# A sigmoid recurrence in chunks of two lengths, with its additions on VectorE and a last attention tile in two unequal parts

## The chip, the cores and the metric

The kernel runs on one core of a Trainium2 chip. The metric is the device time of one execution in microseconds (us), taken as the median of several runs. Engines are named as the profile names them: PE (TensorE), DVE (VectorE), ACT (ScalarE), POOL (GpSimd) and SP (SyncE, which here only issues transfers).

## What is computed

The input is a tensor of 4 batches, 128 channels and 64 x 64 = 4096 positions, all in float32. Layer 0 is a group norm and a full attention over the positions. Layer 1 treats the positions as tokens: a layer norm and a causal attention, then a layer norm and a recurrent block. Each adds its result to its input. The part that the change is about is the end:

```python
x = x + attn0(group_norm(x))                 # 4096 x 4096 scores for each batch
t = tokens(x)                                # (4, 4096, 128)
t = t + causal_attn(layer_norm(t))
Wx = layer_norm(t) @ W.T                     # normalised over all 4 x 4096 tokens
Wx = (Wx - mean) * rsqrt(var + 1e-5) * gamma + beta
def step(yt, wx_t):                          # over the 4096 tokens, y0 = 0
    yt = sigmoid(wx_t + yt @ V.T)
    return yt, yt
t = t + ys
```

## The kernel before

**Attention.** The batches are worked through one after the other, and each batch in its two layers. A layer is cut into 8 tiles of 512 queries. A tile is made of units: a unit takes 256 keys (two blocks of 128), computes their scores on PE (`ps`, L888 in layer 1), the exponentials on ACT (`s`, L901), a running sum of them on DVE (`total`, L929) and their product with the values on PE (`av`, L932). The product of a unit follows the score of the next one in PE's order. Work that belongs to other tiles is put between units by hand: `finish` divides by the sum, projects (`po`) and adds the input; `ffn` then normalises the tokens (`pt_f`, `rstd_f`), multiplies by the recurrent block's weight (`pw_f`, `w_f`), and ACT writes the product into `WX` (L752). Each of these is a generator that does one piece between two units; where it yields, the next unit comes first. In causal tiles POOL sets the upper triangle of the diagonal blocks to zero (L904).

In the last layer of the last batch the order of the tiles is 0, 1, 2, 4, 5, 6, 7, 3, and tile 3 is done in two halves of 256 queries (`LAST = 3`). When all is done, the statistics over all tokens are put together (`fmv`, L981), and from them a `gain` and a `bias`.

**Recurrence.** The 4096 steps are cut into chunks of `CHUNK = 32`, which run side by side: 128 chunks of each batch are the columns of one matmul. The start of a chunk isn't known, so each first runs the last `WARM = 12` steps of the chunk before it from a value of 0.5 into `first`; at the end `ok` compares the value so reached with the one that the neighbour computed, and only where they differ by more than 2e-6 a second, general kernel runs. A chain makes 12 + 32 = 44 steps. There are two chains, of two batches each, so a step of a chain has 256 columns: a matmul with `FV` (L1020) adds to PSUM, where DVE has written `gain * Wx` ahead of it (`seed`, L1010, four steps at once into one of two buffers of the chain), and a sigmoid on ACT (L1021) writes the result into `first` or over `WX`.

`residual` (L1025) adds `WX` to the kept input of the recurrent block (`Y` for batches 0 to 2, `X` for batch 3). The tokens of a chunk lie 32 elements apart there. POOL does it for batches 0 and 1 and most of batch 2 while the steps run; DVE does the last 8 steps of batch 2 and all of batch 3 after them. Then 8 stores of 1 MB go out, half on SP's queue and half on ACT's.

Of the kernel before, what the change touches and what calls it, by code (L numbers as in the profile page):

```python
# [463 lines left out]
CHUNK = 32  # L464
# [5 lines left out]
BL = 4  # L470
LAST = 3
# [3 lines left out]
def fast_kernel(  # L475
# [14 lines left out]
    NP = N // (2 * P)  # L490
    NC = N // CHUNK
    G = 4
    assert C == P and 2 * CQ == P and N % QT == 0 and NC == P
# [60 lines left out]

    WXp = [wxpool.tile([P, 2, CHUNK, NC], F32, name=f"WX{g}") for g in range(B // 2)]
    WX = [WXp[b // 2][:, b % 2] for b in range(B)]
# [6 lines left out]
    with ExitStack() as actx:  # L563
# [172 lines left out]
        def ffn(b, c, off, w):  # L736
            name = f"f_{b}_{c}_{off}"
            cols = ds(c * QT + off, w)
            src = X2[b][:, cols]
            if b < len(kept):  # L740
                nc.sync.dma_start(out=kept[b][:, cols], in_=src)
            yield
            _, _, rstd = deviations(src, 1e-5, name)
            yield
            rb = spread(rstd, name)
            pw = misc(f"pw_{name}")[:, :w]
            nc.tensor.matmul(pw, lhsT=FWc, rhs=src, start=True, stop=True)  # L747
            if off == 0:
                wt[b, c] = tmp.tile([P, QT], F32, tag="w", name=f"w_{name}")
            part = wt[b, c][:, ds(off, w)]  # L750
            nc.vector.tensor_tensor(part, pw, rb, ALU.mult)  # L751
            nc.scalar.copy(  # L752
                WX[b][:, :, ds((c * QT + off) // CHUNK, w // CHUNK)].rearrange("p l s -> p s l"),
                part.rearrange("p (s l) -> p s l", l=CHUNK),
            )
            if off + w == QT:
                nc.vector.bn_stats(stats_f[:, b * NQ + c, :], wt.pop((b, c)))
            yield

        def finish(b, layer, c, off, w, av, total):  # L760
# [24 lines left out]
            yield  # L785
            yield
# [12 lines left out]
        units, following = [], {}  # L799
        for b in range(B):  # L800
            for layer in range(2):
                order = list(range(NQ))
                if (b, layer) == (B - 1, 1):
                    order.append(order.pop(LAST))
                following.update({(b, layer, c): d for c, d in zip(order, order[1:])})
                for c in order:
                    halves = [(0, QT // 2), (QT // 2, QT // 2)] if (b, layer, c) == (B - 1, 1, order[-1]) else [(0, QT)]
                    for off, w in halves:
                        n = (c * QT + off + w) // (2 * P) if layer else NP
                        units += [(b, layer, c, off, w, u, n) for u in range(n)]  # L810
# [22 lines left out]
        def begin_tile(b, layer, c):  # L833

            if layer == 0:
                if c == 0 and b:
                    for k in range(NQ):
                        whole(("k0", b, k))
                    put(("q0", b, 0), query0(b, 0))
                if c == 1 and b == 0:  # L840
                    put(("m1",), merge1())
                if c == 3 and 0 < b < B - 1:
                    for k in range(NQ):
                        whole(("f", b - 1, k, 0))
                    load_x(b + 1)
                if c == (5 if b else 2) and b + 1 < B:
                    put(("gn", b + 1), gn_stats(b + 1))
                if c == NQ - 1:
                    put(("q1", b, 0), after(b, 0))
                whole(("q0", b, c))  # L850
                if c + 1 < NQ:
                    put(("q0", b, c + 1), query0(b, c + 1))
            else:
                if c == 0 and b + 1 < B:
                    whole(("gn", b + 1))
                    for k in range(NQ):
                        put(("k0", b + 1, k), keys0(b + 1, k))
                whole(("q1", b, c))
                if (b, 1, c) in following:
                    d = following[b, 1, c]  # L860
                    todo.insert(0, ("q1", b, d))
                    made["q1", b, d] = after(b, d)
# [9 lines left out]
        def score(i):  # L872
# [11 lines left out]
            first = [max(j0 + h, 0) * P if layer else 0 for h in range(2)]  # L884
            for h in range(2):
# [12 lines left out]
            for h in range(2 if layer else 0):  # L898
# [3 lines left out]
                if j0 >= 0:  # L902
# [7 lines left out]
        def product(i):  # L910
# [7 lines left out]
            both = first[0] == first[1]  # L918
            if u == 0:
                if not both:  # L920
                    nc.vector.memset(total[:, 1, : first[1]], 0.0)
                for h in (slice(0, 2),) if both else range(2):
                    f = 0 if both else first[h]
                    nc.vector.tensor_copy(total[:, h, f:w], s[:, h, f:w])
            else:
                for h in (slice(0, 2),) if both else range(2):
                    f = 0 if both else first[h]
                    t = total[:, h, f:w]
                    nc.vector.tensor_tensor(t, t, s[:, h, f:w], ALU.add)  # L929
            V = V1[b] if layer else V0[b]  # L930
            for h in range(2):
                nc.tensor.matmul(  # L932
                    av[:, first[h] : w], lhsT=V[:, 2 * u + h, :], rhs=s[:, h, first[h] : w],
                    start=u == 0 and h == 0, stop=u == n - 1 and h == 1,
# [6 lines left out]
            if u == n - 1:  # L941
# [28 lines left out]
    with ExitStack() as fctx:  # L970
# [20 lines left out]
        nil = small.tile([P, QT], F32R, name="nil")  # L991
        nc.vector.memset(nil.bitcast(F32), 0.0)
        first = [small.tile([P, 2, NC], F32, name=f"first{g}") for g in range(B // 2)]
        for g in range(B // 2):
            nc.vector.memset(first[g], 0.5)
        steps = list(range(CHUNK - WARM, CHUNK)) + list(range(CHUNK))
        nk = len(steps) // BL
        where = {}

        def seed(g, k):  # L1000
            ps = where[g, k] = ps_y.tile([P, BL, 2, NC], F32, tag=f"y{g}", name=f"py{g}_{k}")
            if k < 2:
                for j in range(0, BL, 2):
                    nc.tensor.matmul(
                        ps[:, j : j + 2].rearrange("p j h s -> p (j h s)"), lhsT=nil[:, :P], rhs=nil,
                        start=True, stop=True,
                    )
            j0, lo = steps[k * BL], int(k * BL < WARM)
            for js in [slice(j, j + 1) for j in range(BL)] if k == 0 else [slice(0, BL)]:
                nc.vector.tensor_scalar(  # L1010
                    ps[:, js, :, lo:].rearrange("p j h s -> p h j s"),
                    WXp[g][:, :, j0 + js.start : j0 + js.stop, : NC - lo], gain, None, ALU.mult,
                )

        def advance(g, k, j):
            n, lo = k * BL + j, int(k * BL < WARM)
            dst = first[g][:, :, 1:] if lo else WXp[g][:, :, steps[n], :]
            y = dst if lo else first[g] if n == WARM else WXp[g][:, :, steps[n] - 1, :]
            ps = where[g, k][:, j, :, lo:]
            nc.tensor.matmul(ps, lhsT=FV, rhs=y, start=False, stop=True, skip_group_check=True)  # L1020
            nc.scalar.activation(dst, ps, AF.Sigmoid, bias=bias)  # L1021

        def residual(eng, b, ls, cols=slice(0, NC)):
            xj = X[b].rearrange("p (s l) -> p l s", l=CHUNK)[:, ls, cols]
            eng.tensor_tensor(xj, xj, WX[b][:, ls, cols], ALU.add)  # L1025

        for k in range(2):
            for g in range(B // 2):
                seed(g, k)
        for k in range(nk):  # L1030
            for j in range(BL):
                for g in range(B // 2):
                    advance(g, k, j)
            if k == WARM // BL - 1:
                for g in range(B // 2):
                    nc.vector.memset(first[g][:, :, 0:1], 0.0)
            for g in range(B // 2 if k + 2 < nk else 0):
                seed(g, k + 2)
            if k * BL >= WARM:
                ls = slice(steps[k * BL], steps[k * BL] + BL)  # L1040
                for b in range(3 if k < nk - 2 else 2):
                    residual(nc.gpsimd, b, ls)
        residual(nc.vector, 2, slice(CHUNK - 2 * BL, CHUNK))
        for h in range(2):
            residual(nc.vector, 3, slice(0, CHUNK), ts(h, NC // 2))
        for b in range(B):
            for h in range(2):
                cols = ts(h, N // 2)
                (nc.scalar if h else nc.sync).dma_start(out=out[b, :, cols], in_=X[b][:, cols])
# [4 lines left out]
        ok = small.tile([P, B, NC], F32, name="ok")  # L1054
        nc.vector.memset(ok, 0.0)
        for b in range(B):
            nc.vector.tensor_tensor(
                ok[:, b, 1:], first[b // 2][:, b % 2, 1:], WX[b][:, CHUNK - 1, : NC - 1], ALU.subtract
            )
# [3 lines left out]
        nc.vector.tensor_reduce(good[:, 0:1], ok.rearrange("p b s -> p (b s)"), AX.X, ALU.min)  # L1063
# [3 lines left out]
        pf = ps_y.tile([P, BL, 2, NC], F32, tag="y0", name="pflag")[:, 0, 0, :]  # L1067
# [52 lines left out]
```

## Time and profile before

| | |
|---|---|
| median of 3 runs | 2593.09 us (2592.93 to 2595.2) |
| profiled execution | 2594.39 us, of which the span is 2592.4 us |
| last product of attention | 2489.0 us |
| gain ready | 2505.5 us |
| first step of the recurrence | 2508.57 us |
| last sigmoid | 2565.1 us |
| last addition of `residual` | 2578.0 us |
| additions on POOL | 22 of 128x512, 1599 ns each |
| additions on DVE | 1 of 128x1024, 2 of 128x2048 |

Places in time are microseconds from the start of the span of the profiled execution. A duration is that of one instruction by the profiler; "x8" means eight of them. Two records make one float32 matmul. In the timeline the last column in brackets is the engine's idle time ahead of the instruction and what ended it.

### The profile page before, as it was taken

Reading aid. Unit: us, or ns where it says so; the run is one execution under the profiler, and the core shown is the slowest. Engines: PE = TensorE matmul, PEld = TensorE weight load, DVE = VectorE, ACT = ScalarE, POOL = GpSimd, SP = SyncE. Lnnn points to the kernel's source line nnn. Section 1 sums busy time; section 2 is a strip of 40 time slices with the busy share of each in tenths; the row PEclk is TensorE's granted clock in tenths of the full one; section 3 lists DMA queues with packets and bytes.
Section 4 is the critical chain, followed back from the end, with each engine's and each line's share of the span. In section 5 each row is a group of like instructions: output and inputs, shape, how many; then the busy total and the mean of one; then the engine's idle time right before and its main releaser. Section 6 shows DMA issues by size and latency. Waiting matters only on the chain.

```text
span 2592.4 us, 21739 instructions
## 1 busy us (share of the span) xinstructions
PE 2519.8 (97%) x7372; PEld 1345.1 (52%) x7372; DVE 1760.3 (68%) x3513; ACT 1139.7 (44%) x1386; POOL 219.7 (8%) x297
## 2 busy tenths in 40 slices
PE   7999999999999999999999999999999999999975
PEld 4555554444555555444555555444455555544552
DVE  7776667567867667666876666765786766776564
ACT  4444444444444444444444444444444444344444
POOL 2010001101000100010100010110100000000005
PEclk9999999999999999999999999999999999999988
DMA  2000000000100000000100000000010000000013
GB/s 72 1 0 1 0 1 13 9 4 4 37 0 1 0 1 5 13 5 8 37 0 1 1 0 1 13 9 5 5 37 0 1 1 1 0 1 1 0 65 131
DMA packets 11943, 31.28 MB, mean 12 GB/s; under 512 B 2096, under 2 KB 2864, under 8 KB 10032
## 3 DMA queue, kind: packets, MB, share of 16 engines
q1 hardware_dynamic: 8928, 24.12, 2.6%
q10 hardware_dynamic: 2896, 5.71, 0.6%
q8 instruction: 59, 0.97, 0.2%
q14 instruction: 60, 0.49, 0.1%
HBM read 15.14 MB, written 14.68 MB: 12 GB/s over the span
## 4 chain that ended last, share of the span: by engine, by line
PE 89%; DVE 6%; issue 2%; ACT 1%; POOL 1%; DMA 0%; SPq 0%; POOLq 0%; ACTq 0%; DVEq 0%
PE av L932 48%; PE ps L895 17%; PE ps L888 17%; PE po L788 2%; DVE total L929 1%; PE py L1020 1%; PE pq L730 1%; PE pk L649 1%; POOL rstd_f L561 1%; PE pw_f L747 1%; ACT WX L1021 1%; PE pt L688 1%; DVE lst_f L692 0%; PE pt L665 0%; DVE w_f L751 0%
## 5 line engine op out<-in xcount | busy, mean ns | idle before, releaser
L929 DVE TENSOR_TENSOR total<-total,s 128x1024 f32<-128x1024 f32 (+4 forms) x802 | 881.6, 1103 | 553.4 <-ACT s L897 308.9
L932 PE MATMUL av<-s,WX 128*128 128x512 f32 x2048 | 964.4, 593 | 3.4 <-ACT s L897 3.4
L897 ACT ACTIVATE s<-ps,shift 128x1024 f32<-128x1024 f32 x512 | 569.2, 1114 | 772.9 <-PE ps L895 749.0
L895 PE MATMUL ps<-q,K 128*128 128x512 f32 x2048 | 759.7, 493 | 2.1 <-DVE K L660 1.5
L901 ACT ACTIVATE s<-ps,zero,R 128x512 f32<-128x512 f32 (+1 forms) x590 | 399.9, 729 | 458.9 <-PE ps L888 458.3
L932 PEld LDWEIGHTS av<-s,WX 128*128 128x128 f32 x2048 | 382.2, 189 | 312.0 <-issue 270.0
L895 PEld LDWEIGHTS ps<-q,K 128*128 128x128 f32 x2048 | 386.7, 189 | 291.0 <-issue 236.3
L932 PE MATMUL av<-s,V 128*128 128x512 f32 (+3 forms) x1180 | 504.7, 549 | 0.6 <-ACT s L901 0.6
L888 PE MATMUL ps<-q,X 128*128 128x512 f32 (+3 forms) x1180 | 501.9, 548 | 0.0
L888 PEld LDWEIGHTS ps<-q,X 128*128 128x128 f32 x1180 | 222.6, 190 | 239.7 <-issue 228.2
L932 PEld LDWEIGHTS av<-s,V 128*128 128x128 f32 x1180 | 218.8, 191 | 226.1 <-issue 201.6
L561 POOL TENSOR_TENSOR rstd<-rstd,mhalf 128x4 f32<-128x4 f32 x32 | 32.7, 1022 | 1015.5 <-DVE rstd L560 1015.5
L904 POOL TENSOR_SCALAR_AFFINE_SELECT s<-s 128x128 f32<-128x128 f32 x128 | 46.5, 367 | 523.0 <-ACT s L901 522.4
L646 POOL TENSOR_SCALAR X<-X,B0v 128x512 f32<-128x512 f32 x32 | 59.6, 1865 | 243.8 <-DVE xg L644 238.1
L794 DVE SCALAR_TENSOR_TENSOR X<-po,X 128x512 f32<-128x512 f32 (+1 forms) x65 | 44.1, 678 | 51.3 <-PE po L788 50.9
L752 ACT COPY WX<-w_f 128x512 f32<-128x512 f32 (+1 forms) x33 | 35.3, 1069 | 93.1 <-DVE w_f L751 93.1
L561 POOL TENSOR_TENSOR rstd_f<-rstd_f,mhalf 128x4 f32<-128x4 f32 (+1 forms) x33 | 36.1, 1094 | 398.6 <-DVE rstd_f L560 398.6
L721 DVE TENSOR_SCALAR V<-pt,lmv,rstd 128x128 f32<-128x128 f32 x128 | 43.7, 404 | 35.8 <-POOL rstd L561 35.8
L788 PE MATMUL po<-o,W1v 128*128 128x512 f32 (+1 forms) x66 | 34.4, 604 | 16.1 <-DVE o L782 16.1
L679 DVE TENSOR_TENSOR q<-QR,qh 64x512 fp32r<-64x512 f32 x64 | 43.9, 685 | 6.3 <-PE ps L895 5.7
L765 DVE TENSOR_TENSOR t<-total 128x512 f32<-128x512 f32 (+1 forms) x65 | 44.5, 684 | 4.5 <-PE pfw L605 2.5
L782 DVE SCALAR_TENSOR_TENSOR o<-rb,av 128x512 f32<-128x512 f32 (+1 forms) x65 | 43.9, 675 | 4.4 <-DVE rb L780 0.5
(124 smaller groups left out, 1312.5 us busy)
## 6 DMA issues: line engine op xcount, KB each, us to landing
X<-in_x SPq DMA_DIRECT2D x28, 256.0 KB, 5.5
kept<-X SPq DMA_DIRECT2D x24, 256.0 KB, 2.0
Y<-kept SPq DMA_DIRECT2D x6, 1024.0 KB, 7.6
out<-Y SPq DMA_DIRECT2D x3, 1024.0 KB, 9.7
out<-Y ACTq DMA_DIRECT2D x3, 1024.0 KB, 10.2
X<-in_x ACTq DMA_DIRECT2D x4, 256.0 KB, 5.6
out<-X SPq DMA_DIRECT2D x1, 1024.0 KB, 16.1
out<-X ACTq DMA_DIRECT2D x1, 1024.0 KB, 12.6
```

Of the source, the lines that this page charges most:

```text
L561: nc.gpsimd.tensor_tensor(dst, dst, mhalf[:, :n], ALU.pow)
L646: nc.gpsimd.tensor_scalar(xt, xt, B0v, None, ALU.add)
L765: nc.vector.tensor_tensor(t, total[:, 0, :w], total[:, 1, :w], ALU.add)
L788: nc.tensor.matmul(po, lhsT=W1v if layer else W0v, rhs=o, start=True, stop=True)
L794: nc.vector.scalar_tensor_tensor(dst, po, 1.0 / GUARD, xt, ALU.mult, ALU.add)
L888: nc.tensor.matmul(ps[:, h, first[h] : w], lhsT=lhsT, rhs=q[:, off + first[h] : off + w], start=True, stop=True,)
L895: nc.tensor.matmul(ps[:, h, :], lhsT=lhsT, rhs=q[:, k, :], start=k == 0, stop=k == 1)
L897: nc.scalar.activation(s, ps, AF.Exp, bias=shift)
L901: nc.scalar.activation(part, ps[:, h, first[h] : w], AF.Exp, scale=scale, bias=zero)
L904: nc.gpsimd.affine_select(out=edge, in_=edge, pattern=[[1, P]], base=0, channel_multiplier=-1, compare_op=ALU.is_ge, fill=0.0,)
L929: nc.vector.tensor_tensor(t, t, s[:, h, f:w], ALU.add)
L932: nc.tensor.matmul(av[:, first[h] : w], lhsT=V[:, 2 * u + h, :], rhs=s[:, h, first[h] : w], start=u == 0 and h == 0, stop=u == n - 1 and h ...
```

## The change

- Batches 0 and 1 are now cut into chunks of 16 steps, batches 2 and 3 still into chunks of 32. There are three chains: batch 0 alone (256 chunks, 12 + 16 = 28 steps), batch 1 alone (the same), and batches 2 and 3 together (2 x 128 chunks, 44 steps). After the 28th step the two batches of the third chain make their steps separately, with 128 columns each.
- `seed` writes two steps at once for the first two chains and four for the third; the first one isn't cut into single steps any more.
- All additions of `residual` are on DVE: four steps of batches 0 and 1 after each fourth step, eight steps of batches 2 and 3 at a time later, and the last eight in two pieces of four.
- The stores of batches 0 and 1 are issued on SP as soon as their additions are done; those of batches 2 and 3 at the end, half on SP and half on ACT.
- The tiles of the last layer run in their natural order, and the last one (tile 7) is split into 384 and 128 queries. A part can have an odd number of key blocks, so its last unit may have one block. For a part narrower than 512 `finish` yields five times ahead of `po` instead of twice.
- `nil` (zeros, which open the PSUM banks) is made once at the start with 128 columns and read four times over; the memsets of `first` and `ok` move from DVE to POOL.

```diff
-CHUNK = 32
+CHUNK = (16, 16, 32, 32)
-BL = 4
-LAST = 3
+LAST = 384
...
-            yield
-            yield
+            for _ in range(2 if w == QT else 5):
+                yield
             po = misc(f"po_{name}")[:, :w]
...
-                order = list(range(NQ))
-                if (b, layer) == (B - 1, 1):
-                    order.append(order.pop(LAST))
...
+                for c in range(NQ):
+                    parts = [(0, LAST), (LAST, QT - LAST)] if (b, layer, c) == (B - 1, 1, NQ - 1) else [(0, QT)]
+                    for off, w in parts:
+                        n = (c * QT + off + w) // P if layer else NB
+                        units += [(b, layer, c, off, w, u, n) for u in range((n + 1) // 2)]
...
+        chains = (((0,), 2), ((1,), 2), ((2, 3), 4))
...
+            nc.vector.tensor_scalar(
+                ps[:, :, :, lo:].rearrange("p j h s -> p h j s"), src[:, :, j0 : j0 + bl, : NC[b] - lo],
+                gain, None, ALU.mult,
+            )
...
+            parts = [slice(h, h + 1) for h in range(2)] if n >= len(steps[0]) else [slice(0, len(bs))]
+            for hs in parts:
...
+                nc.tensor.matmul(ps, lhsT=FV, rhs=y, start=False, stop=True, skip_group_check=True)
+                nc.scalar.activation(dst, ps, AF.Sigmoid, bias=bias)
+
+        def residual(b, l, n):
+            xj = X[b].rearrange("p (s l) -> p l s", l=CHUNK[b])[:, l : l + n, :]
+            nc.vector.tensor_tensor(xj, xj, WX[b][:, l : l + n, :], ALU.add)
+
+        def store(b, h):
+            (nc.scalar if h and b > 1 else nc.sync).dma_start(out=out[b, :, ts(h, N // 2)], in_=X[b][:, ts(h, N // 2)])
...
-            for g in range(B // 2 if k + 2 < nk else 0):
-                seed(g, k + 2)
-            if k * BL >= WARM:
-                ls = slice(steps[k * BL], steps[k * BL] + BL)
-                for b in range(3 if k < nk - 2 else 2):
-                    residual(nc.gpsimd, b, ls)
-        residual(nc.vector, 2, slice(CHUNK - 2 * BL, CHUNK))
-        for h in range(2):
-            residual(nc.vector, 3, slice(0, CHUNK), ts(h, NC // 2))
...
+        late = [(b, l) for l in range(0, CHUNK[2] - 8, 8) for b in (2, 3)]
+        for n in range(len(steps[2])):
+            for g in range(3):
+                advance(g, n)
...
+            for g, (_, bl) in enumerate(chains):
+                if (n + 1) % bl == 0:
+                    seed(g, (n + 1) // bl + 1)
+            if WARM < n < last and (n + 1) % 4 == 0:
+                for b in range(2):
+                    residual(b, n - WARM - 3, 4)
+                if n == last - 1:
+                    for b in range(2):
+                        for h in range(2):
+                            store(b, h)
+            elif n >= last and late and WARM + late[0][1] + 8 <= n:
+                residual(*late.pop(0), 8)
+        for b, l in late:
+            residual(b, l, 8)
+        for l in (CHUNK[2] - 8, CHUNK[2] - 4):
+            for b in (2, 3):
+                residual(b, l, 4)
+        for b in (2, 3):
+            for h in range(2):
+                store(b, h)
```

## The prediction

> **What bounds the kernel now.** I read the page first, then a table of busy time by stage, then the chain of waits and the timeline of the last 110 us.
>
> ```profile
> PE 2519.8 (97%) x7372; PEld 1345.1 (52%) x7372; DVE 1760.3 (68%) x3513; ACT 1139.7 (44%) x1386; POOL 219.7 (8%) x297
> ```
>
> TensorE (PE) is busy 97% of the span, in attention, which the change leaves alone up to the last tile. What it touches lies in the stages after 2460 us (columns: stage, length, busy time of PE, weight loads, DVE, ACT, POOL, clock, DMA share, GB/s):
>
> ```profile
> 2460.00:2489.00 29.00, 26.42 (x118) 21.93 (x116) 19.96 (x62) 14.86 (x28) 2.68 (x6) 0.94 0.00 1
> 2489.00:2508.50 19.50, 6.52 (x15) 3.81 (x14) 14.84 (x59) 1.55 (x4) 1.96 (x3) 0.65 0.54 215
> 2508.50:2565.10 56.60, 52.73 (x176) 27.13 (x176) 25.06 (x23) 41.13 (x87) 31.07 (x20) 0.97 0.00 0
> 2565.10:2578.00 12.90, 0.26 (x2) 0.00 (x0) 12.88 (x6) 0.47 (x1) 3.23 (x2) 0.61 0.81 335
> 2578.00:2588.00 10.00, 0.59 (x2) 0.50 (x2) 2.62 (x8) 0.00 (x0) 0.00 (x0) 0.50 0.99 406
> ```
>
> The stages are: end of attention; its epilogue on DVE; 44 steps of the recurrence; what is left of the additions on DVE (12.88 of 12.90 us busy); the rest of the stores, with DMA full. The end follows at 2592.4. In the chain of waits a step looks like this:
>
> ```profile
> 2526.76 0.71 PE py L1020 x2
> 2527.47 0.02 issue
> 2527.49 0.48 ACT WX L1021
> 2527.98 0.04 issue
> 2528.02 0.71 PE py L1020 x2
> ```
>
> One step costs 1.26 us, a matmul and a sigmoid in turn; two chains alternate in it, so ACT is used 2 x 0.475 = 0.95 us of 1.26. 44 x 1.26 = 55.4. Last the timeline behind the steps:
>
> ```profile
> 2565.12 1.85 DVE L1057 TENSOR_TENSOR ok<-first,WX 128x127 f32<-128x127 f32 x2 [7.64 <-ACT WX L1021]
> 2565.17 3.23 POOL L1025 TENSOR_TENSOR Y<-Y,WX 128x512 f32<-128x512 f32 x2 [1.93 <-ACT WX L1021]
> 2566.86 3.81 SPq L1049 DMA_DIRECT2D out<-Y  x3
> ...
> 2566.89 3.41 DVE L1025 TENSOR_TENSOR Y<-Y,WX 128x1024 f32<-128x1024 f32 x1
> 2570.13 7.85 DVE L1025 TENSOR_TENSOR X<-X,WX 128x2048 f32<-128x2048 f32 x2
> ```
>
> Two additions of 2048 elements took 7.85 us, **1.9 ns an element**; the one of 1024, counted from 2568.4 when POOL's ended, took 1.7 to 1.9. This price decides the case.
>
> **What the Trainium skill says.** "SBUF — State Buffer", Who interferes with whom: a DVE instruction with two SBUF inputs and a POOL one that reads SBUF shut each other out. The trace agrees: the two small `ok` subtractions took 1.85 us beside POOL's addition, and two later ones 0.50. So additions moved from POOL must be paid on DVE, but nothing blocks them there. The same page, The DMA port swizzle, says that SBUF lines have 16 bytes and each access to a new line costs extra; both strides of the additions (64 and 128 bytes) then cost alike. The trace agrees on 64 bytes for a read, without DMA beside it:
>
> ```profile
> L775 DVE TENSOR_REDUCE z<-side 32x16 f32<-32x64 f32 x63 | 15.1, 239 | 1.4
> L775 DVE TENSOR_REDUCE z<-side 32x8 f32<-32x32 f32 x2 | 0.3, 172 | 0.0
> ```
>
> (239 - 172) / 32 = 2.1 ns an element, where the contiguous reduction of L769 pays (673 - 402) / 256 = 1.06. "TensorE: Matmul & The Clock Gate", LDWEIGHTS: a load of 128 columns takes 128 / 1.2 = 107 ns; its records here last 190 ns but may overlap, since four 128-wide transposes came in 0.44 us. Same page, What's actually happening: after some 3.4 us idle PE runs at half clock. The clock of 0.65 in the epilogue agrees.
>
> **The change part by part.** Times are against the span of the profiled run.
>
> 1. *Last tile in 384 and 128.* PE's columns stay the same: a unit (two 128-row blocks, scores and products) takes 3.44 us at 512 columns, 1.72 at 256, so 0.86 at 128. The 128 part has 16 units: 13.8 us, with 1.6 for the first part's `po`, `pt_f`, `pw_f`. But a score must pass ACT first: two exps of 128 (450 ns each, 0.35 apart) and the drain come to about 1.0 us after the score, against 0.86 of other PE work, so some 0.1 us a unit is lost: +1.5. DVE has 15 to 17 us in that time, about as long as PE. Before, PE lost 2.6 us to `o` and some 1.4 to the half clock after it. The three more yields move `po` behind units that cover DVE's `o`. Net **-1** (-3 to +3; rival 2 beyond that).
>
> 2. *Epilogue.* Before: from the last product to `w_f` 13.7 us, since the first half's ffn shares DVE with the second half's finish. Now only 128 columns are left: `t` to `o` 15 instructions of 0.15 to 0.3 us, 3.2 with gaps (7.4 before); `po` 1.1 (1.3); `X` to `w_f` 4.3 (5.2); with the last addition 9.1. **-4.6** (-3 to -6). Statistics and gain (2.9 us) stay. The memsets of 0.5 and of `ok` go to POOL, which idles.
>
> 3. *First step.* Before, PE's first step waited for seven of eight seeds, 3.0 us after the gain. Now one seed of 510 elements (0.67 us by the 0.386 of 254 and 1.24 of 1016) and the bias are enough: 0.9. **-2.1**.
>
> 4. *Steps and additions.* Three chains of 256 columns for 28 steps: ACT 3 x 0.475 = 1.43 us a step, PE 1.29, round trip 1.26, so 1.43. The 16 steps after that run in halves of 128 on two chains: about 1.0 each. ACT and PE alone would need 28 x 1.43 + 16 = 56, as before. But DVE now does all additions: 4 x 4096 elements x 1.9 ns = 31 us, of which it did 5120 elements before and POOL 11264 beside the steps. The first can start after step 15, 16 x 1.43 + 0.5 = 23.4 us from the first step. From there DVE's queue holds 14 additions of 1024 (1.96 us), four of 512 (0.99), nine seeds of 512 (0.67), six of 1024 (1.24) and three `ok` (0.3): 27.4 + 4.0 + 6.0 + 7.4 + 0.9 = 45.7 us. It doesn't idle: seeds stand in its order behind additions, and PE and ACT, which take their steps in order, wait for them. The seed of steps 20 and 21 comes behind two additions (about 1.5 us late), that of 24 behind two more, that of steps 36 to 39 behind five (some 5 us). So the last addition ends 23.4 + 45.7 = 69.1 us after the first step, plus 1.5 for PE's half clock at the start (six records of 0.43 instead of 0.215 for some two steps): 70.6. Before it was 2578.0 - 2508.6 = 69.4. **+1.2**. The gain of shorter chunks goes into the wait for seeds.
>
> 5. *Stores.* Batches 0 and 1 go out 47 and 50 us after the first step (23.4, seven or eight additions and the seeds among them), on SP, with nothing behind them but the last stores; 4.19 MB at 418 GB/s last 10 us and are over by 61. Batches 2 and 3 cannot start before their last additions. The halves of 2 are issued 1.3 us before the last addition ends, and 4.19 MB take 10.0: -1.3 + 0.7 + 10.0 = 9.4 us, where before 10.2 us of stores were left at 2578.0. **-0.8**. The 4.2 us at the end stay.
>
> Chunk sizes in ACT's `WX` copies (16 for 32) hide under PE's 97%; if not, 16 copies by 0.1 us.
>
> Sum: -1 - 4.6 - 2.1 + 1.2 - 0.8 = **-7.3 us**. The profiled run took 2594.39 (span 2592.4 and 2.0 around it) and would take 2587.1; the median of the runs is 1.3 lower, 2593.09, so I predict 2585.8, rounded to 2586. A measurement of this kernel can tell about 0.2% (5.2 us) from no change.
>
> **The rivals.**
>
> *1. The additions are cheap.* If the 1.9 ns came from the stores that ran beside both measured additions, they cost what the contiguous total of L929 does, 1.2 ns. DVE saves 16384 x 0.7 = 11.5 us, of which about 10 show, as steps then take over as the bound: 2576. For it: no addition of the trace ran without DMA. Against it: L775. Halfway if only the 64-byte stride is cheap: 2580.
>
> *2. Weight loads bound the 128 part.* 128 records at 190 ns are 24.3 us instead of 13.8; 1.5 is paid already: +9, so 2595. For it: the length of the records. Against it: the transposes.
>
> *3. The additions are dear, and the kernel slower.* VectorE pays for X's stride what POOL did, 1599 ns for 512, 3.1 ns an element: 16384 x 1.2 = +19.7, so 2605. It decides from 1.9 + 7.3 / 16.4 = 2.35 ns on (slower), 2.65 (by over 0.2%). For it: rows of 256 were never added. Against it: the three prices above.
>
> *4. The early store does nothing.* So I forecast: it is worth 0.8 us, as the last stores wait for DVE. If DMA were the bound, as rival 1 brings nearer, it would be worth more. That the convergence test `ok` fails with more chunk borders and the general kernel runs too is excluded at 1%: the 12 warm steps stay.
>
> **How the numbers follow.** Forecast 0.57 (its own range 2579 to 2592 from points 1, 2 and 4 at 1.8 to 2.1 ns), of which 0.42 is faster by over 0.2% and 0.15 within; rival 1 0.20, all faster; rival 2 0.08, within 0.07; rival 3 and what I don't see 0.15, slower 0.14. So faster 0.62, same 0.22, slower 0.16. The range 2575 to 2596 leaves out half of rival 1's lower side and most of rival 3.
>
> **What would show it.** Right: DVE nearly full from step 15 to the last addition with rows of 128x1024 near 1.96 us; steps waiting for `py` seeds, the longest wait before step 36; the first step about 8 us earlier; DMA idle between two bursts of 10 us. Wrong: additions at 1.2 us (rival 1) or 3 (rival 3); L929 records of 128 columns 0.19 apart (rival 2); a first step less than 5 us earlier.

## The result: slower by 0.15%, and the profile after

| | before | changed |
|---|---|---|
| median | 2595.07 us (2591.53 to 2596.02) | 2598.28 us (2595.76 to 2599.73) |
| ratio | | 1.0015, 95% interval 1.0008 to 1.0023 |
| span of the profiled execution | 2592.4 us | 2596.0 us |

The loss is real, though under the 0.2% named ahead; I forecast 2586 us, 0.28% faster, and the time lies above the range that I gave. Here are the milestones of the two profiled executions, as the lengths between them:

| from, to | before | changed | difference | predicted |
|---|---|---|---|---|
| start, last product | 2489.01 | 2490.59 | +1.6 | -1 |
| last product, gain | 16.52 | 11.58 | -4.9 | -4.6 |
| gain, first step | 3.04 | 0.95 | -2.1 | -2.1 |
| first step, last addition | 69.41 | 78.93 | **+9.5** | **+1.2** |
| last addition, end | 14.42 | 13.95 | -0.5 | -0.8 |

The differences sum to +3.6, which is the difference of the spans. One row carries the miss. Of the first row's +1.6 only 0.2 lies in the attention that the change touches (shown at e12 below); the rest arose in the 2230 us ahead of it, whose length scatters by 3 us from execution to execution. The page's engine line moves little, because all that stands behind attention is 4% of the span:

```profile
PE 2527.9 (97%) x7496; PEld 1363.4 (53%) x7496; DVE 1784.7 (69%) x3544; ACT 1150.3 (44%) x1431; POOL 186.2 (7%) x280
```

The table by stage of the changed kernel shows it (stage, length, busy time of PE, weight loads, DVE, ACT, POOL, clock, DMA share, GB/s). The stages are the end of attention, the epilogue, the first 28 steps, the last 16 steps, and the end:

```profile
2460.00:2490.60 30.60, 28.33 (x174) 22.71 (x172) 18.59 (x54) 19.61 (x43) 2.49 (x5) 1.00 0.00 1
2490.60:2503.10 12.50, 5.28 (x13) 3.59 (x14) 8.65 (x39) 1.00 (x3) 2.59 (x6) 0.62 0.84 336
2503.10:2544.50 41.40, 38.11 (x169) 27.87 (x168) 37.99 (x42) 35.96 (x84) 0.00 (x0) 0.99 0.00 1
2544.50:2580.90 36.40, 23.13 (x64) 15.00 (x64) 24.77 (x18) 12.18 (x33) 0.00 (x0) 0.55 0.28 115
2580.90:2596.00 15.10, 0.59 (x2) 0.50 (x2) 4.28 (x9) 0.00 (x0) 0.00 (x0) 0.50 0.70 283
```

The 28 steps take 41.4 us; I had 28 x 1.43 + 1.5 = 41.5, which agrees by luck: most rounds of the three chains take 1.29 us, and two of them 3.1 to 3.2, where PE waits for a seed. The 16 steps after them take 36.4 where I had 16, and in them no engine is full: PE 23.1, DVE 24.8, ACT 12.2 of 36.4 us, with PE's clock near a half. When no engine is full, they must be waiting for each other. The chain of waits says which (start, length, engine, tile, line):

```profile
2546.44 0.50 PE py L1033 x2
2546.97 0.38 ACT WXp L1034
2547.35 0.04 issue
2547.39 0.50 PE py L1033 x2
...
2549.59 0.81 PE py L1033 x2
2550.43 0.38 ACT WXp L1034
2550.80 0.04 issue
2550.85 0.81 PE py L1033 x2
```

Each pair is one *half* of a step (128 columns). So the halves run one after the other: 0.95 us each while the clock is full, 1.25 from 2548.3 on, 1.9 to 2.5 us a step. The table of waits between 2544 and 2581 us (total, times, longest) agrees: nearly every matmul waits for a sigmoid, and every sigmoid for its matmul.

```profile
ACT WXp L1034 <- PE py L1033: 23.9, 28, 0.9
PE py L1033 <- ACT WXp L1034: 12.8, 28, 0.5
DVE Y L1038 <- ACT WXp L1034: 11.5, 3, 6.8
```

The third line is the reversal of my forecast: DVE, whose queue I let set the end, waits 11.5 us for the steps. The timeline at the end shows its last and longest wait in brackets, and then stores as predicted:

```profile
2579.68 1.14 DVE L1038 TENSOR_TENSOR Y<-Y,WXp 128x512 f32<-128x512 f32 x1 [6.81 <-ACT WXp L1034]
...
2580.93 1.12 DVE L1038 TENSOR_TENSOR X<-X,WXp 128x512 f32<-128x512 f32 x1
...
2582.08 0.33 SPq L1041 DMA_DIRECT2D out<-X  x1
```

The price on which the case was to be decided held. The groups by shape (busy time, mean ns of one):

```profile
L1038 DVE TENSOR_TENSOR Y<-Y,WX 128x1024 f32<-128x1024 f32 x8 | 15.5, 1995 | 0.0
...
L1038 DVE TENSOR_TENSOR X<-X,WXp 128x1024 f32<-128x1024 f32 x3 | 6.5, 2178 | 0.0
```

1.9 to 2.1 ns an element, with the 1.9 forecast: rivals 1 (1.2) and 3 (3.1) are out. The first seven of the eight began before any store was issued (2547.7), so the stores are not what makes them dear.

### The profile page after: what moved, and what is told of

It is laid out like the page before. It is cut to its first block, busy times and chain, and to the rows that moved or that the text cites. A ratio compares the mean times of both kernels' runs of the same rounds, so it can differ in the third digit from the quotient of the medians.

```text
span 2596.0 us, 22075 instructions
## 1 busy us (share of the span) xinstructions
PE 2527.9 (97%) x7496; PEld 1363.4 (53%) x7496; DVE 1784.7 (69%) x3544; ACT 1150.3 (44%) x1431; POOL 186.2 (7%) x280
## 4 chain that ended last, share of the span: by engine, by line
PE 88%; DVE 6%; ACT 2%; issue 2%; POOL 1%; POOLq 0%; DVEq 0%; ACTq 0%
PE av L929 47%; PE ps L891 17%; PE ps L884 17%; PE po L789 2%; DVE total L926 2%; PE pq L731 1%; PE py L1033 1%; PE pk L650 1%; POOL rstd_f L562 1%; PE pw_f L748 1%; PE pt L689 1%; DVE lst_f L693 1%; ACT WXp L1034 1%; PE pt L666 0%; DVE w_f L752 0%
## 5 line engine op out<-in xcount | busy, mean ns | idle before, releaser
L926 DVE TENSOR_TENSOR total<-total,s 128x1024 f32<-128x1024 f32 (+5 forms) x810 | 882.9, 1094 | 548.4 <-ACT s L893 309.9
L929 PE MATMUL av<-s,WXp 128*128 128x512 f32 x2048 | 963.9, 593 | 4.5 <-ACT s L893 4.5
L897 ACT ACTIVATE s<-ps,zero,R 128x512 f32<-128x512 f32 (+3 forms) x607 | 404.4, 717 | 452.9 <-PE ps L884 451.4
L929 PEld LDWEIGHTS av<-s,WXp 128*128 128x128 f32 x2048 | 382.0, 189 | 313.4 <-issue 270.1
L562 POOL TENSOR_TENSOR rstd_f<-rstd_f,mhalf 128x4 f32<-128x4 f32 (+2 forms) x33 | 35.8, 1085 | 411.4 <-DVE rstd_f L561 411.4
L766 DVE TENSOR_TENSOR t<-total 128x512 f32<-128x512 f32 (+1 forms) x65 | 44.4, 683 | 4.5 <-PE pfw L606 2.5
L768 DVE STREAM_TRANSPOSE tt<-t 128x512 f32<-128x512 f32 (+1 forms) x65 | 45.5, 700 | 1.7
L781 DVE STREAM_TRANSPOSE rb<-z 128x512 f32<-128x512 f32 (+1 forms) x65 | 45.4, 698 | 1.2
## 6 DMA issues: line engine op xcount, KB each, us to landing
out<-X SPq DMA_DIRECT2D x1, 1024.0 KB, 11.5
```

The costliest lines, as they stand in the source:

```text
L562: nc.gpsimd.tensor_tensor(dst, dst, mhalf[:, :n], ALU.pow)
L768: nc.vector.transpose(tt, t)
L781: nc.vector.transpose(rb, z[:, :k].unsqueeze(2).to_broadcast([P, k, 32]))
L897: nc.scalar.activation(part, ps[:, h, first[h] : w], AF.Exp, scale=scale, bias=zero)
L929: nc.tensor.matmul(av[:, first[h] : w], lhsT=V[:, 2 * u + h, :], rhs=s[:, h, first[h] : w], start=u == 0 and h == 0, stop=2 * u + h == n - 1,)
```

## The experiments

Two kinds of number are used: the ratio of times to the kernel before, and the length from the first step to the last addition in the profiled execution. The second is the sharper one. Eleven of the kernels (the changed one and e1 to e10) contain the same new attention, and their profiled executions end it between 2488.1 and 2491.4 us, so two single spans compare only to about 3 us. The five whose steps run as in the changed kernel (it, e2, e4, e8, e12) agree in the length within 0.3 us, 78.9 to 79.2.

**e1_whole: no halves.** The third chain steps with 256 columns to its end.

```diff
-            parts = [slice(h, h + 1) for h in range(2)] if n >= len(steps[0]) else [slice(0, len(bs))]
+            parts = [slice(0, len(bs))]
```

> The changed kernel, but the third chain makes its last 16 steps with both batches at once (256 columns) instead of one batch after the other (2 x 128). Theory A (the two halves write and read one PSUM bank, so PE and ACT must take turns and a step costs 2.2 us instead of the 1.0 I wrote): the 16 steps become 1.26 us each while PE is at full clock, 1.95 (2 x 0.71 + 0.48) where it is at half clock, so 20 to 31 us instead of 35.1. At the low end DVE's queue bounds: 21.9 us to its first addition + 46.4 us of its own work, last addition about 68 us after the first step instead of 78.8, about 2588 us. At the high end (half clock in most of the steps) about 2594. Theory B (the halves don't matter, DVE's queue is what ends last): within 2 us of the changed kernel, 2596 to 2600. Theory C (only PE's half clock makes the steps slow, whatever their width): steps near 1.95, 2594.

Measured: 2589.66 us, ratio 0.9983 (0.9977 to 0.9990); first step to last addition 71.3 us. So the halves cost 78.9 - 71.3 = 7.6 us, and without them the change is a gain. Theory B is out. The time lies between the two ends that I gave, since the half clock plays a part; but the half clock alone (theory C) is not the cause, as at the same half clock a whole step takes 1.8 us here (below) and its two halves took 2.5. The stage table of e1:

```profile
2548.00:2560.00 12.00, 7.99 (x14) 3.26 (x14) 12.00 (x8) 2.84 (x6) 0.00 (x0) 0.50 0.82 341
```

And its timeline at the end of the steps:

```profile
2571.55 1.13 DVE L1038 TENSOR_TENSOR Y<-Y,WXp 128x512 f32<-128x512 f32 x1 [4.32 <-ACT WXp L1034]
```

At clock 0.50 a step's matmul takes 1.22 us, and with the sigmoid a step 1.8. DVE is full to 2567.2, then waits 4.3 us for the last steps. A single chain cannot be faster than its round trip, so splitting was a sound idea; its execution is what failed.

**e2_banks: one bank for each half.** The first theory was that the halves share a PSUM bank. "PSUM — Partial Sum Buffer", PSUM bank collisions raise a hardware error, of the Trainium skill says that two engines must not use one bank on the same partitions at the same time, and that ordering must therefore go by bank, not by address. None of these runs shows such an error. In the tile `[P, 4, 2, 128]` both halves of a step do lie in one bank. Here they get one each:

```diff
-            ps = where[g, k] = ps_y.tile([P, bl, m, NC[b]], F32, tag=f"y{g}", name=f"py{g}_{k}")
+            if k * bl < len(steps[0]):
+                ps = ps_y.tile([P, bl, m, NC[b]], F32, tag=f"y{g}", name=f"py{g}_{k}")
+            else:
+                ps = ps_y.tile([P, m, bl, NC[b]], F32, tag=f"y{g}", name=f"py{g}_{k}").rearrange("p h j s -> p j h s")
+            where[g, k] = ps
```

> The changed kernel with its halves of 128 columns, but for the last 16 steps the PSUM tile of the third chain is laid out batch by batch, so that batch 2 has one bank and batch 3 the other. Instructions, widths and order stay. Theory A (one bank for both halves is the cause): the halves now overlap, PE is busy nearly all the time (4 records of about 0.25 us a step), so it stays at full clock and a step is about 1.0 us, 16 us for the 16 steps; DVE's queue then ends last, last addition about 68 us after the first step, about 2588 us. Rival (PE's half clock, or the round trip of narrow steps, makes 2.2 us a step): nothing changes, 2596 to 2600, clock 0.50 after 2550.

Measured: 2597.7 us, ratio 1.0015 (1.0008 to 1.0022); first step to last addition 79.1. Nothing changed, and the timeline of e2 shows the same turns:

```profile
2544.13 0.49 PE L1037 MATMUL py<-WXp,FV 128*128 128x128 f32 x2 [0.46 <-ACT WXp L1038]
2544.66 0.37 ACT L1038 ACTIVATE WXp<-py,fbias 128x128 f32<-128x128 f32 x1 [0.58 <-PE py L1037]
...
2545.08 0.49 PE L1037 MATMUL py<-WXp,FV 128*128 128x128 f32 x2 [0.46 <-ACT WXp L1038]
```

So the first theory, as stated, fell: banks of their own are not enough. A half still waits for the sigmoid of the *other* half, with which it shares neither data nor bank, but a tile.

The changed kernel's own trace agrees. Its tile holds four steps, two in each of its two banks. Between steps 31 and 32 one tile gives way to the next, and there the second half of the one and the first half of the other follow each other without a wait, four records and then two sigmoids:

```profile
2552.10 1.22 PE L1033 MATMUL py<-WXp,FV 128*128 128x128 f32 x4 [0.46 <-ACT WXp L1034]
...
2552.93 0.79 ACT L1034 ACTIVATE WXp<-py,fbias 128x128 f32<-128x128 f32 x2 [0.89 <-PE py L1033]
```

It is the same at the next two borders of tiles (2561.30 and 2570.50). Between steps 29 and 30 (2548.34), where the bank changes inside a tile, a half waits for the other as everywhere else.

**e5_tiles: one tile for each half**, from step 32 on, in the buffers of the two finished chains. With the tile the seed is split, too: two of 512 elements for one of 1024. In the changed kernel no half waited for a seed.

```diff
+            if k * bl > len(steps[0]):
+                where[g, k] = []
+                for h in range(2):
+                    ps = ps_y.tile([P, bl, 1, NC[b]], F32, tag=f"y{h}", name=f"py{g}{h}_{k}")
...
+                    where[g, k].append(ps)
+                return
...
-                ps = where[g, n // bl][:, n % bl, hs, lo:]
+                ps = where[g, n // bl]
+                ps = ps[hs.start][:, n % bl] if isinstance(ps, list) else ps[:, n % bl, hs, lo:]
```

> The changed kernel with its halves of 128 columns, but from step 32 of the third chain on each half has a PSUM tile of its own (the buffers that the two short chains have left), and its own seed of 512 elements; steps 28 to 31 stay as they were. e2 laid the halves in two banks of one tile and nothing changed: in its trace each half still waited for the sigmoid of the other. Theory A' (it is the tile, by which the order of PE's writes and ACT's reads is kept, that makes the halves take turns): from step 32 on they overlap, a half still has 0.49 PE + 0.37 ACT + 0.1, so a step takes about 1.0 us at full clock and 1.3 at half clock, and the 16 steps 4 x 2.2 + 12 x 1.0 to 1.3 = 21 to 24 us instead of 35.1; the last addition comes 66 to 70 us after the first step, 2585 to 2589 us. Rival (a half-width step costs 2.2 us for another reason, such as ACT taking turns anyway): 2596 to 2600.

Measured: **2584.87 us, ratio 0.9965 (0.9951 to 0.9978)**; first step to last addition 66.7 us, 12.2 less than the changed kernel. The timeline of e5, where PE's records now merge into one block and sigmoids come in pairs:

```profile
2549.59 6.86 PE L1044 MATMUL py<-WXp,FV 128*128 128x128 f32 x21 [0.46 <-ACT WXp L1045]
...
2550.42 0.80 ACT L1045 ACTIVATE WXp<-py,fbias 128x128 f32<-128x128 f32 x2 [0.89 <-PE py L1044]
...
2551.67 0.79 ACT L1045 ACTIVATE WXp<-py,fbias 128x128 f32<-128x128 f32 x2 [0.46 <-PE py L1044]
```

A step of both halves takes 1.25 us, though PE is at half clock; before it was 2.5. DVE is now full from 2525 to 2567. The cause is settled: in this program the order of matmuls and sigmoids is kept by PSUM tile, and two chains in one tile are one chain. The SBUF tile `WXp`, which both halves read and write, isn't it, as they still share it in e5. What two tiles in one bank would do wasn't tried; each half of e5 has a bank of its own, too.

**e3_tile: the last attention tile alone**, with the recurrence of before (the diff is that of `units`, `finish` and `LAST` above).

> The kernel before with the new last tile alone (384 and 128 queries, natural order, five yields), its recurrence, additions and stores as they were. If the milestones of the changed kernel add up: the last product 1.6 us later, the epilogue 4.9 us shorter, so 3.3 us faster than before, 2591.8 us (ratio 0.9987). My prediction's steps 1 and 2 had -5.6. Rival (the shorter epilogue is given back, since the recurrence's seeds or PE's clock start later): no gain, 2595.

Measured: 2591.63 us, ratio 0.9988 (0.9982 to 0.9995), -3.1 us (-1.3 to -4.7). The parts add up: this gain is kept in the changed kernel, and the recurrence turns it into a loss.

**e4_late and e8_hold: what the early stores are worth.**

```diff
-                if n == last - 1:
-                    for b in range(2):
-                        for h in range(2):
-                            store(b, h)
...
-        for b in (2, 3):
+        for b in (2, 3, 0, 1):
             for h in range(2):
                 store(b, h)
```

> The changed kernel with the four stores of batches 0 and 1 issued behind those of batches 2 and 3, at the end. If the early stores are worth what DMA takes for 4.19 MB (10 us at 418 GB/s): 10 us slower than the changed kernel, 2608. If they are worth nothing (rival 4): 2598.

Measured: 2596.78 us in one run, no change; but its trace still issues those stores from 2546.4 on, while the steps run. A store's place in SP's queue isn't set by the place of its call, so this run says nothing of rival 4. e8 makes them depend on batch 3's last addition:

```diff
+                one = X[b][:, h * N // 2 : h * N // 2 + 1]
+                nc.vector.scalar_tensor_tensor(one, X[3][:, N - 1 : N], 0.0, one, ALU.mult, ALU.add)
                 store(b, h)
```

> The changed kernel with the stores of batches 0 and 1 really held until all additions are done (a tiny DVE instruction that reads batch 3's last column and adds 0 times it to batch 0's and 1's; in e4_late the stores were written later in the program but stood in the same place of SP's queue). If the early stores are worth DMA's time for 4.19 MB: 8 to 10 us slower than the changed kernel, 2606 to 2608. If they are worth nothing (rival 4): 2598.

Measured: 2606.22 us in one run, and from the last addition to the end 23.85 us instead of 13.95. In this comparison of two profiled executions the early stores are worth 9.9 us, DMA's time for their 4.19 MB.

**e6_order: fewer stores behind the last addition.** To e5's edit comes (`residual` has the column half as a fourth argument; both stores of batch 2 follow its last addition):

```diff
-        late = [(b, l) for l in range(0, CHUNK[2] - 8, 8) for b in (2, 3)]
+        late = [(2, 0), (3, 0), (2, 8), (3, 8), (2, 16)]
...
+        residual(2, 24, 8)
...
+        for h in range(2):
+            residual(3, 16, 16, h)
+            store(3, h)
```

> As e5_tiles, and the additions of the end in another order: batch 2 is completed first and stored, then batch 3's last 16 steps in two column halves, each stored when done. So 1 MB instead of 4 MB is stored behind the last addition. If DVE's additions and the stores behind them are what ends last (theory A'): the last addition as in e5, and 14.0 us behind it become about 7 to 8 (2.5 for 1 MB, what is left of the stores before it, 4 at the end), so 5 to 7 us faster than e5, 2579 to 2583 us. Rival (the stores are held by DMA or by the issue, not by DVE's order): no gain over e5.

Measured: 2585.75 us, ratio 0.9967 (0.9955 to 0.9979), the same as e5. The tail did shrink, from 14.05 to 11.1 us, but the additions grew from 66.7 to 70.6. In e6's timeline DVE waits for the last step, and then has 6 us of additions where e5 had kept 1.5 back:

```profile
2566.74 2.07 DVE L1050 TENSOR_TENSOR Y<-Y,WXp 128x1024 f32<-128x1024 f32 x1 [3.50 <-ACT WXp L1045]
2568.72 4.00 DVE L1050 TENSOR_TENSOR X<-X,WXp 128x1024 f32<-128x1024 f32 x2
```

**e7_pool: the additions of batches 0 and 1 on POOL**, else as e5.

```diff
-            nc.vector.tensor_tensor(xj, xj, WX[b][:, l : l + n, :], ALU.add)
+            (nc.gpsimd if b < 2 else nc.vector).tensor_tensor(xj, xj, WX[b][:, l : l + n, :], ALU.add)
```

> As e5_tiles, with the 8 additions of batches 0 and 1 on POOL (128x1024 each, 3.2 us by the 1.6 us that 512 elements cost it before), those of batches 2 and 3 on DVE. If POOL and DVE shut each other out in these additions (theory A', with the Trainium skill's rule): 25.6 us on POOL from 2525 and 16 us on DVE cannot overlap and end near 2567, about the 2569 of e5, so 2584 to 2590 us, with DVE additions far longer than 2.0 us while POOL works. Rival (they overlap): POOL ends near 2551, DVE's 16 us begin before it, the last addition follows the last sigmoid, 2578 to 2583 us.

Measured: 2594.32 us, ratio 0.9999 (0.9990 to 1.0007); first step to last addition 74.7, 8 worse than e5 and outside both expectations. From e7's timeline:

```profile
2524.78 17.20 POOL L1049 TENSOR_TENSOR Y<-Y,WX 128x1024 f32<-128x1024 f32 x6 [22.59 <-ACT WX L1045]
...
2534.15 9.81 DVE L1049 TENSOR_TENSOR Y<-Y,WXp 128x1024 f32<-128x1024 f32 x1
...
2544.70 1.19 PE L1044 MATMUL py<-WX,FV 128*128 128x256 f32 x2 [6.69 <-DVE py L1023]
```

One DVE addition of 2 us lasted 9.8 and ended at 2544.0, 2 us after POOL's sixth. What I left out is what stands behind it: a seed, for which PE waited 6.7 us and fell to half clock (1.19 us for two records). The exclusion does not only shift the additions, it stops the steps. DVE's order differs as well: its first addition of batch 2 stands 31 us after the first step here and 48 us in e5, and how much of the 8 us that order costs isn't shown. With e5's steps, the additions of batches 0 and 1 are better on DVE.

**e9_all, e10_early: is DVE's queue the bound of e5?** e9 gives all 16 steps their own tiles, with the seed of steps 28 to 31 written after step 25; e10 also starts the additions two steps earlier (from `if WARM` on). The diff is against e5.

```diff
-            if k * bl > len(steps[0]):
+            if k * bl >= len(steps[0]):
...
-                if (n + 1) % bl == 0:
+                if (n + 1) % bl == 0 and (g, n) != (2, 23):
                     seed(g, (n + 1) // bl + 1)
+            if n == 25:
+                seed(2, 7)
-            if WARM < n < last and (n + 1) % 4 == 0:
+            if n in (13, 17, 21, 25, 27):
                 for b in range(2):
-                    residual(b, n - WARM - 3, 4)
+                    m = 2 if n in (13, 27) else 4
+                    residual(b, n - WARM - m + 1, m)
```

> As e5_tiles, with the tiles of their own from step 28 on (the seed of steps 28 to 31 is written two steps later for that, when a buffer is free), so that all 16 steps overlap and none of them runs in turns. Theory A': all 16 steps cost 1.0 (full clock) to 1.25 us (half clock), 16 to 20 us instead of the 21.7 of e5; the last sigmoid comes 2 to 5 us earlier, but DVE was full in e5 to its last addition, so the end moves by 0 to -1 us only: 2584 to 2585. It also shows whether PE's clock stays at 1.0 when the four slow steps are gone. Rival (the steps and not DVE's queue ended last in e5): 2 to 4 us faster than e5, 2581 to 2583.

> As e9_all, with the additions of batches 0 and 1 in pieces of 2, 4, 4, 4 and 2 steps instead of four times 4, so that DVE starts its first two steps earlier. If DVE's queue, full from its first addition on, is what ends last: two steps earlier is 2 x 1.3 = 2.6 us, less 0.2 for two more instructions, so 2.4 us faster than e9, about 2582. Rival (steps or stores end last): no gain over e9.

Measured: e9 2587.13 us, ratio 0.9972 (0.9961 to 0.9984), first step to last addition 66.6; e10 2585.86, ratio 0.9969 (0.9958 to 0.9980), 65.6. In e9 the first eight of the steps took 8.49 us, 1.06 each, and the time gained was waited for at the ninth (e9's timeline):

```profile
2545.12 8.49 PE L1044 MATMUL py<-WXp,FV 128*128 128x128 f32 x32 [0.92 <-DVE py L1008]
...
2557.40 10.20 PE L1044 MATMUL py<-WXp,FV 128*128 128x128 f32 x32 [3.79 <-DVE py L1008]
```

PE waits for the seed of step 36, which stands behind additions on DVE: the wait that the prediction named. So faster steps alone gain nothing, and the rival is out. But e5 is bound by both: DVE is busy 44.4 of 44.5 us from its first addition to its last, and yet its chain of waits goes through the steps from 2542 to 2565, most of them at half clock, and its last addition of batch 2 starts 0.03 us after the sigmoid that it needs. Of e10's 2.4 us one came in the length (its first addition is only 1.6 us earlier than e9's), and nothing that the times can tell. Behind the last addition e9 took 16.2 us and e10 15.0, where e5 took 14.05; no run here says why.

**e11_best, e12_copy: the ACT copy between two exponentials.** In the changed kernel PE waited 1.93 us near the end of attention, because ACT's copy of the 384 part waits for DVE's `w_f` in front of an exponential. e12 is the changed kernel with that copy on POOL, e11 adds it to e10.

```diff
-            nc.scalar.copy(
+            (nc.gpsimd.tensor_copy if w == LAST else nc.scalar.copy)(
```

> As e10_early, and ACT's copy of the last tile's 384 part into WX is done on POOL instead, so that it doesn't stand between two exponentials of a unit and wait for DVE's w_f there (PE waited 1.9 us for it at 2486 to 2488 in the changed kernel). If that wait is what made the attention end 1.6 us later instead of 1 us earlier: the last product about 1.9 us earlier and so is all behind it, 1.9 us faster than e10, about 2580. Rival (POOL's copy holds DVE's running sum, which has two inputs in SBUF, for as long): no gain over e10.

> The changed kernel with that copy on POOL alone. The last product of attention at about 2488.7 us of the span instead of 2490.6, the end about 1.9 us earlier than the changed kernel's, 2594 to 2596.5 in one run. Rival: the last product stays at 2490 to 2491.

Measured: e11 2585.76 us, ratio 0.9969 (0.9956 to 0.9981), no gain over e10; e12 2597.53 in one run, last product at 2489.84, inside the 2488.1 to 2491.4 of the kernels that kept the copy on ACT. By these numbers alone one execution differs from the next by more than the effect. The traces do show it when the length is counted from the first score of the last causal attention (batch 3) to its last product. It is 256.6 us in the kernel before (from 2232.37), 256.9 in ten of the eleven kernels with the new tile and the copy on ACT (257.2 in e10), and 255.4 in both e11 and e12. PE's longest wait near the end, in the changed kernel and in e12, shows where it comes from:

```profile
2487.90 0.49 PE L929 MATMUL av<-s,V 128*128 128x128 f32 x2 [1.93 <-ACT s L897]
...
2488.40 0.49 PE L929 MATMUL av<-s,V 128*128 128x128 f32 x2 [0.54 <-ACT s L897]
```

So the copy on POOL is worth 1.5 us of the 1.9 expected. What hid half of it in e12 is the stretch ahead: that execution began its last attention at 2234.44, the changed kernel at 2233.71.

e5, e6, e9, e10 and e11 all beat both kernels, with ratios of 0.9965 to 0.9972 that the intervals don't tell apart; e5 has the lowest median and the smallest edit.

## Why the prediction was wrong, point by point

1. **Last tile, -1: wrong, +0.2**, counted within the last causal attention (e12 above); the +1.6 of the table holds 1.3 us from the stretch ahead of it, which took 2231.2 to 2234.5 us in the kernels with this attention. I put ACT's copies into `WX` at nothing. One of them stands in front of an exponential and makes PE wait 1.93 us; without it (e11, e12) the tile is at -1.2. Rival 2 is out: from 2474 to 2476 us the scores and products of the 128 part follow each other at 0.45 us for four records, 0.11 each and not 0.19.
2. **Epilogue, -4.6: right**, -4.9, and 11.5 to 11.6 us in all kernels with the new recurrence (12.4 in e3, whose memsets are still on DVE). e3 shows that the gain of 1 and 2 together reaches the time.
3. **First step, -2.1: right**, -2.1.
4. **Steps and additions, +1.2: wrong, +9.5.** The failed term is "the 16 steps after that run in halves of 128 on two chains: about 1.0 each". I priced each engine's share of a step and took it that the halves overlap, without asking what keeps PE's write and ACT's read of one tile apart. They take turns: 36.4 us for the 16 steps, 2.3 each. e5, which changes only that (with the seeds) from step 32 on, has 66.7 us in place of 78.9. The rest of the term held: DVE full from 22.0 us after the first step to 2559, steps waiting for seeds behind additions, 1.9 to 2.1 ns an element. The wait ahead of step 36, which I had as the longest, comes only where the steps are fast enough for it, in e9. e5's 66.7 is even 3.9 below my 70.6: its first addition comes at 22.3 us and not at 24.9, and its queue lasts 44.4 us and not 45.7. The first is a size that I had wrong: sigmoids begin 0.43 us apart, before the record of 0.475 of the one ahead has ended, so a round takes PE's 6 x 0.215 = 1.29 us and not 3 x 0.475. That e5's ratio, worth -9.1 us, is near the -7.3 that I forecast for the change is partly luck: the queue came out 3.9 better and the last tile 1.2 worse than I wrote. In the kernel before, the last sigmoid ended at 2565.9 and not at 2565.1, so its steps took 57.3 us where I wrote 56.
5. **Stores, -0.8: right**, -0.5. The 0.8 compares with the kernel before, which issues six of its eight stores at 2566.9, 11 us ahead of its last addition; set against a version of the changed kernel that really holds the stores (e8), the early ones are worth 9.9 us.

The rival on the slower side sat in the wrong place. I gave it to DVE's price; the loss came from a wait that the trace before cannot show, because there no two chains share a tile.

## What to carry to other kernels

When a chain is split so that its parts may overlap, check that each part has its own PSUM tile and not only its own columns or bank; a profile in which two engines alternate and neither is full is a sign that it hasn't. Price a split by its round trip both overlapped and in turns, before adding up busy times. And what an addition on POOL costs is more than its own length: in e7 the dear part was what queued behind the DVE instruction that it blocked.

## What the runs showed of the hardware that I had not expected

- PE's clock did not recover though PE counts as busy: in e5's stage table PE is busy 11.90 of 12.00 us and the clock stays at 0.50. The ends of its records are modelled, and they hide pauses: the records start 0.23 to 0.37 us apart, waiting for sigmoids, where records of that shape in the last attention tile, at clock 1.00, start 0.11 apart.

```profile
2552.00:2564.00 12.00, 11.90 (x40) 9.38 (x39) 12.00 (x11) 7.02 (x20) 0.00 (x0) 0.50 0.46 192
```

- Two sigmoids of 128x256 that follow each other take 0.91 us together in the trace: they start 0.43 apart, at PE's pace, while one record lasts 0.475. So the sum of ACT's records, 3 x 0.475, made my round of three chains too long.
- DVE's addition of 1024 elements takes 1.96 to 2.03 us in batches 0 and 1 (64 bytes apart, rows of 256) and 2.11 to 2.21 in batches 2 and 3 (128 bytes, rows of 128); I had taken them to cost alike. Stride and rows changed together, so which of them costs isn't shown.
